# Image 0 loaded and normalised ahead of the tables of relative logits; the taps of the convolution and the second layer's weights asked for last

## The chip, the cores and the metric

The kernel runs on one core of a Trainium2 chip. The metric is the time of one launch in microseconds of the device. Before the change it is 2572.06 us, the median of five runs (2569.28 to 2577.38).

## The reference

A batch of 8 images, 32 x 32 pixels, 256 channels, float32, goes through two layers.

```python
# layer 0: group norm (32 groups), then a hybrid of convolution and attention, and a residual
x = x + concat[ conv3x3(gn(x)) + conv_b   (192 channels),
                attn(gn(x)) @ attn_w + attn_b   (64 channels) ]
#   attn: kqv = gn(x) @ qkv_w + qkv_b; 8 heads of 8; 1024 x 1024 logits per head,
#   logits = q k + rel_w + rel_h     (relative logits from key_rel_w, key_rel_h, 63 x 8 each)
# layer 1: attention of one head of 128 over the 1024 tokens, projected back, two residuals
t = t + (softmax(Q K / sqrt(128)) V) @ W_o + b_o + ln(t)
# then a feed-forward of 2 of 8 experts per image, chosen from the mean token, and a layer norm
t = t + layer_norm(experts(ln(t)) + ln(t)) * gamma + beta
```

## The kernel before, in words

Everything before the experts is one stage with eight rounds, one for each image; the experts are a second stage with eight rounds. In the first stage TensorE's instructions run in the order in which the program lists them (`manual_schedule` for that engine); the other engines' instructions are ordered by the framework's planner, so their order on the chip can differ from the program's. Within one engine instructions run in order, and one that waits holds all behind it.

The part in question is the head, ahead of image 0's first scores.

- *Loads.* `load_image(0)` (L105) loads image 0, 1 MB, on POOL's queue. ScalarE's queue loads `qkvw` (L121, 192 KB) and the convolution's `taps` (L125, 1728 KB). SP's queue loads in this order: `kqb`, `vb`, `l0b` in two parts, `aw`, the three of `wqkv1`, `wo`, `bo` (L139 to L158), and then the two raw tables `rawh` and `raww` (L181, 2 KB each).
- *Taps.* The 3 x 3 convolution is computed for pairs of pixels from sums and differences of the taps: three VectorE operations, a scaling, and two ScalarE copies make `convw` (L130 to L135).
- *Selectors* made of the identity: `gsel`, `gavg`, `esel`, `hsel`.
- *Tables.* For each of the two raw tables: a VectorE copy `rep` (L185), a TensorE transpose `relt` (L187), four VectorE writes (L194) to `bdh` or `bdw`. Then `reld`: 16 pieces, half on VectorE and half on POOL (L205, L208).
- *Key patterns.* `oh` on VectorE (L220 to L222) and 32 POOL operations that fill `km0` and `km1` (L228, L229).
- *Image 0's normalisation,* `norm_steps(0)`: 16 transposes (L270), copies to `xT` (L271), statistics (L275 to L296, with one square root on ScalarE), and the normalised, padded image `gpad` (L299, two VectorE operations). In between POOL adds the bias `l0b` to the image (L279).
- `by_tiles`: POOL copies `gpad` to tiles `x` (L320). `by_pairs`: `gdif`, sums and differences of neighbouring pixels, half on VectorE and half on POOL (L311).
- `input_steps(0)`: matmuls `pk` (L334), ScalarE and VectorE write `kq` (L343, L346), SP's queue writes the keys into `km` (L358, 16 transfers), matmuls `pvv` (L367) that read the tiles `x`, matmuls `prel` (L406) that read `bdw`, then `reld`, evicted to `rw` and `rh` (L418, L420), `rw` sent to DRAM (`rwd`, L423), transposes `tpw` (L431), and unit 0's loads of `F` (L484, L488, L495).
- Then the rounds. Each image has four units of 8 steps, each with scores `lg` (L512) whose maximum VectorE takes (L520), weights `st` (L552) and sums `po` (L569); the convolution's matmuls `pc` (L452), which read `convw` and `gdif`, fill in, and so does the next image's normalisation near the end of a round.

TensorE's order in the head is: relth, reltw, image 0's transposes and the statistics' two small matmul pairs, pk, pvv, prel, tpw, pc. The tiles `taps`, `x`, `rw` and `F` share three buffers; `rep`, `bdh` and `xT` share four.

Of the kernel before, what the change touches and what calls it, by code (L numbers as in the profile page):

```python
# [9 lines left out]
FP = mybir.dt.float32  # L10
I32 = mybir.dt.int32
AF = mybir.ActivationFunctionType
ALU = mybir.AluOpType
# [3 lines left out]
P = 128  # L17
# [3 lines left out]
KC = C // P  # L21
NH, DH, DK = 8, 8, 64
HG = 4
NG = NH // HG
CO = C - DK
U = 128
E, F = 8, 512
# [8 lines left out]
def kernel(  # L36
# [26 lines left out]
    nc = tc.nc  # L63
    xt = x.rearrange("b h w c -> b (h w) c")
# [12 lines left out]
    ident = const.tile([P, P], FP, tag="ident", name="ident")  # L77
# [13 lines left out]
    with ExitStack() as ph:  # L91
        wp = ph.enter_context(tc.tile_pool(name="wp", bufs=1))
        work = ph.enter_context(tc.tile_pool(name="work", bufs=1))
# [8 lines left out]

        def load_image(b):
            t = work.tile([P, NT, C], FP, tag="T", name="T", bufs=2)
            nc.gpsimd.dma_start(out=t.rearrange("p (r j) c -> p r j c", j=2), in_=xt[b].rearrange("(r p j) c -> p r j c", p=P, j=2))  # L105
            return t

        T = {0: load_image(0)}
# [7 lines left out]
        def st_tile(name):  # L116
            return ps_st.tile([P, 512], FP, tag="st", name=name)


        qkvw = wp.tile([P, KC, 3 * DK], FP, tag="qkvw", name="qkvw")  # L120
        nc.scalar.dma_start(out=qkvw, in_=qkv_w.rearrange("(k p) o -> p k o", p=P))  # L121


        taps = work.tile([P, 4096], FP, tag="F", name="taps", bufs=3)[:, 0 : 9 * KC * CO]
        nc.scalar.dma_start(  # L125
            out=taps.rearrange("p (n o) -> p n o", o=CO), in_=conv_w.rearrange("a b (k p) o -> p (a b k) o", p=P)
        )
        taps = taps.rearrange("p (a b n) -> p b a n", a=3, b=3)
        convw = wp.tile([P, 4, 3, KC * CO], FP, tag="convw", name="convw")
        nc.vector.tensor_tensor(convw[:, 2], taps[:, 0], taps[:, 2], ALU.add)  # L130
        nc.vector.tensor_tensor(convw[:, 0], convw[:, 2], taps[:, 1], ALU.add)
        nc.vector.tensor_tensor(convw[:, 1], convw[:, 2], taps[:, 1], ALU.subtract)
        nc.vector.tensor_scalar(convw[:, 0:2], convw[:, 0:2], 0.5, None, ALU.mult)
        nc.scalar.copy(convw[:, 2], taps[:, 0])
        nc.scalar.mul(convw[:, 3], taps[:, 2], -1.0)  # L135
        convw = convw.rearrange("p v a (k o) -> p v a k o", o=CO)

        kqb = wp.tile([P, 1], FP, tag="kqb", name="kqb")
        nc.sync.dma_start(out=kqb, in_=qkv_b[0 : 2 * DK].rearrange("(p o) -> p o", o=1))  # L139
# [7 lines left out]
        l0b = wp.tile([P, 1, C], FP, tag="l0b", name="l0b")  # L147
        nc.sync.dma_start(out=l0b[:, 0, 0:CO], in_=conv_b.partition_broadcast(P))
        nc.sync.dma_start(out=l0b[:, 0, CO:C], in_=attn_b.partition_broadcast(P))
        aw = wp.tile([DK, DK], FP, tag="aw", name="aw")  # L150
        nc.sync.dma_start(out=aw, in_=attn_w)
        wqkv1 = wp.tile([P, 3, KC, U], FP, tag="wqkv1", name="wqkv1")
# [3 lines left out]
        nc.sync.dma_start(out=wo, in_=w_o)  # L156
        bo = wp.tile([P, 1, C], FP, tag="bo", name="bo")
        nc.sync.dma_start(out=bo[:, 0, :], in_=b_o.partition_broadcast(P))  # L158

# [11 lines left out]
        hsel = wp.tile([P, HG], FP, tag="hsel", name="hsel")  # L173
        nc.vector.tensor_reduce(hsel, esel.rearrange("p (h d) -> p h d", d=DH), AX.X, ALU.add)


        rel = []
        for n, table in (("h", key_rel_h), ("w", key_rel_w)):
            M = table.shape[0]
            raw = wp.tile([M, DH], FP, tag=f"raw{n}", name=f"raw{n}")  # L180
            nc.sync.dma_start(out=raw, in_=table)  # L181
            rep = work.tile([P, 2048], FP, tag="pt", name=f"rep{n}", bufs=4)[0:M, 0:P].rearrange(
                "m (r d) -> m r d", d=DH
            )
            nc.vector.tensor_copy(rep, raw.unsqueeze(1).to_broadcast([M, P // DH, DH]))  # L185
            pt = st_tile(f"relt{n}")
            nc.tensor.transpose(pt[:, 0:M], rep.rearrange("m r d -> m (r d)"), ident[0:M, 0:M])  # L187
            if n == "h":
                bd = work.tile([P, 2048], FP, tag="pt", name="bdh", bufs=4)[:, 0 : M * HG]
                bd = bd.rearrange("p (m h) -> p m h", h=HG)  # L190
            else:
                bd = wp.tile([P, M, HG], FP, tag="bdw", name="bdw")
            for h in range(HG):
                nc.vector.tensor_scalar(bd[:, :, h], pt[:, 0:M], hsel[:, h : h + 1], None, ALU.mult)  # L194
            rel.append(bd)
        bdh, bdw = rel
        bdw = bdw.rearrange("p m h -> p (m h)")

        def half_w(rows, m, k):
            return bdw[rows, (m + 16 * k) * HG : (m + 16 * k + 16) * HG]  # L200


        NM = 48
        reld = wp.tile([P, NM, 16, HG], FP, tag="reld", name="reld")
        nc.gpsimd.tensor_copy(reld[:, :, 0, :], bdh[:, 0:NM, :])  # L205
        for j in range(1, 16):
            eng = nc.vector if j % 2 else nc.gpsimd
            eng.tensor_tensor(reld[:, :, j, :], bdh[:, j : j + NM, :], bdh[:, 0:NM, :], ALU.subtract)  # L208
        reld = reld.rearrange("p m j h -> p m (j h)")

        def half_h(rows, m, k):
            return reld[rows, m + 16 * k, :]

        KM = []
        oh = wp.tile([P, 16 + DH], FP, tag="oh", name="oh")
        nc.vector.tensor_copy(oh[:, 0:1], esel[:, 0:1])  # L220
        nc.vector.tensor_tensor(oh[:, 1:16], esel[:, 1:16], esel[:, 0:1].to_broadcast([P, 15]), ALU.add)
        nc.vector.tensor_copy(oh[:, 16:24], esel[:, 24:32])  # L222
        for i in range(NG):
            km = wp.tile([P, 2, 4, P], FP, tag=f"km{i}", name=f"km{i}")
            for a in range(2):
                kv = km[:, a].rearrange("p g (y x) -> p g y x", y=8)
                for g in range(4):
                    nc.gpsimd.tensor_copy(kv[:, g], oh[:, 0:16].unsqueeze(1).to_broadcast([P, 8, 16]))  # L228
                    nc.gpsimd.tensor_tensor(  # L229
                        kv[:, g], kv[:, g], oh[:, 16:24].unsqueeze(2).to_broadcast([P, 8, 16]), ALU.add  # L230
                    )
            KM.append(km)

        mcols = []
        for i in range(2):
# [21 lines left out]

        def f_tile(name):
            return work.tile([P, 2, 4, 512], FP, tag="F", name=name, bufs=3)


        def norm_steps(b):
# [50 lines left out]
        def by_tiles():  # L313

            xn = f_tile("x").rearrange("p a e s -> p (a e s)")[:, 0 : KC * S]
            xn = xn.rearrange("p (k j t) -> p k j t", k=KC, j=NT)
            for kc in range(KC):
                for a in range(2):
                    for e in range(4):
                        nc.gpsimd.tensor_copy(  # L320
                            xn[:, kc, a * 4 + e].rearrange("p (y x) -> p x y", y=8),
                            gpad[:, kc, 1 + 16 * a : 17 + 16 * a, 1 + 8 * e : 9 + 8 * e],
                        )
            return dict(xn=xn)
# [551 lines left out]
        with tc.manual_schedule(engines={mybir.EngineType.PE}):  # L876
            held = {}
            for _ in norm_steps(0):
                pass
            held.update(by_tiles())  # L880
            by_pairs()
            for _ in input_steps(0, held):
                pass
            conv = Conv(0)
            means = []
            for b in range(B):
                last = b + 1 == B
                if not last:
                    T[b + 1] = load_image(b + 1)

                def early():
                    if means:
                        token_mean(*means.pop())

                def ahead():

                    yield from norm_steps(b + 1)
                    held.update(by_tiles())
                    by_pairs()

                now, held = held, {}
                conv.place[0] = st_tile
                conv_layer_attention(
                    b,
                    *(now[k] for k in ("units", "kq", "rh", "rwd", "rwq")),
                    conv,
                    early,
                    iter(()) if last else ahead(),
                )
                conv = Conv(b + 1)  # L910
                steps = iter(()) if last else input_steps(b + 1, held)

                def fill(us):

                    while us > 0:
                        took, small = next(steps, (None, None))
                        if took is None:
                            break
                        us -= took
                        if small:  # L920
                            conv.run(3)

                means.append((b, *attention_layer(b, fill, conv.whole)))
                fill(1000.0)
                del T[b]
            token_mean(*means.pop())
# [268 lines left out]
```

## Time and profile before

| | us |
|---|---|
| median of five runs | 2572.06 |
| the profiled execution | 2578.39 |
| its span, first to last instruction | 2576.6 |
| TensorE busy (share of the span) | 2432.7 (94%) |
| VectorE busy | 1412.1 (55%) |
| ScalarE busy | 977.4 (38%) |
| POOL busy | 407.9 (16%) |
| image 0's load issued | 1.50 |
| taps landed, by the wait that ends with them | 16.59 |
| first transpose of image 0 | 20.20 |
| first pk | 46.65 |
| first load of F issued | 67.24 |

The profile is of one execution; times within it are counted from its first instruction. Busy times count instructions, not transfers. The chain of work that ended last is followed back from the last instruction to whatever released each step, and in it a transfer appears as "DMA". A wait is named after what released it last. In rows of a tile or of a line the three durations are the least, the median and the largest, in ns; the three times from DMA to landing are in us.

### The profile page before, as it was taken

How to read it: one execution, taken by the hardware profiler on the slowest of the kernel's cores; microseconds unless marked ns; L12 is line 12 of the kernel's file. 1: busy time of each engine (PE TensorE's matmuls, PEld its weight loads, DVE VectorE, ACT ScalarE, POOL GpSimd, SP SyncE). 2: the span in 40 equal slices, each digit the busy share in tenths (PEclk: the TensorE clock that was granted, in tenths of full speed). 3: DMA queues.
4: the chain of work that ended last, by engine and by line, in shares of the span. 5: the costliest groups of instructions: out<-in, count | busy, mean ns of one | idle time of the engine just before them, and what ended most of it. 6: DMA issues, size and time to landing. Idle time of an engine off the chain costs nothing.

```text
span 2576.6 us, 42566 instructions
## 1 busy us (share of the span) xinstructions
PE 2432.7 (94%) x17769; PEld 1379.8 (54%) x17769; DVE 1412.1 (55%) x2507; ACT 977.4 (38%) x1617; POOL 407.9 (16%) x440
## 2 busy tenths in 40 slices
PE   3999999999999999999999999999998599999998
PEld 2734753575356436643763376347534366666665
DVE  5575477447744873586367537754772623333332
ACT  1055325532643363346225622553264222222222
POOL 6002120302030103202120212030201211111110
PEclk9899999989999999999999999999998799999999
DMA  2430242024203410440044024302420302112100
GB/s 81 90 62 6 51 94 42 23 34 100 37 22 58 86 26 22 83 80 7 28 93 69 3 48 89 52 7 50 83 37 2 108 28 70 72 72 72 66 37 21
DMA packets 73518, 135.87 MB, mean 53 GB/s; under 512 B 12000, under 2 KB 24168, under 8 KB 71280
## 3 DMA queue, kind: packets, MB, share of 16 engines
q1 hardware_dynamic: 67408, 114.42, 21.2%
q0 software_dynamic: 3328, 16.78, 1.9%
q8 instruction: 140, 2.29, 0.4%
q10 hardware_dynamic: 2592, 1.97, 0.3%
q14 instruction: 50, 0.41, 0.1%
HBM read 53.43 MB, written 25.17 MB: 31 GB/s over the span
## 4 chain that ended last, share of the span: by engine, by line
PE 85%; DVE 7%; ACT 4%; DMA 3%; issue 1%; POOL 0%; ACTq 0%; DVEq 0%; SPq 0%
PE lg L512 15%; PE pc L452 10%; PE po L569 9%; PE py L1125 9%; PE phd L1107 9%; PE st L552 8%; PE po L784 4%; PE lg L753 3%; PE prel L406 3%; PE pq L716 2%; PE tp L773 2%; DVE my L520 2%; DMA F<-mb 2%; PE py L1122 2%; ACT PT L560 1%; PE pk L334 1%
## 5 line engine op out<-in xcount | busy, mean ns | idle before, releaser
L560 ACT ACTIVATE PT<-st 128x512 f32<-128x512 f32 (+1 forms) x944 | 541.6, 633 | 582.2 <-PE st L552 579.8
L520 DVE TENSOR_REDUCE my<-lg 128x32 f32<-128x1024 f32 x512 | 617.8, 1223 | 160.6 <-PE st L552 126.5
L552 PE MATMUL st<-F,km 32*128 32x512 f32 x2048 | 549.2, 638 | 14.6 <-DMA F<-mb 8.8
L512 PE MATMUL lg<-km,F 24*128 24x512 f32 x2048 | 528.0, 637 | 0.9 <-DMA F<-rh 0.9
L452 PE MATMUL pc<-convw,gdif 128*128 128x192 f32 x1536 | 308.7, 344 | 10.6 <-DVE T L467 10.6
L569 PE MATMUL po<-PT,vall 128*32 128x256 f32 (+1 forms) x3200 | 313.5, 451 | 3.0 <-ACT PT L560 2.4
L452 PEld LDWEIGHTS pc<-convw,gdif 128*128 128x128 f32 x1536 | 250.8, 193 | 79.8 <-issue 73.4
L512 PEld LDWEIGHTS lg<-km,F 24*128 24x128 f32 x2048 | 151.6, 183 | 176.4 <-issue 101.7
L1125 PE MATMUL py<-w,hT 128*128 128x256 f32 x1024 | 237.3, 385 | 0.0
L569 PEld LDWEIGHTS po<-PT,vall 128*32 128x32 f32 x3200 | 66.8, 108 | 313.9 <-issue 279.1
L552 PEld LDWEIGHTS st<-F,km 32*128 32x128 f32 x2048 | 179.3, 183 | 91.5 <-issue 41.7
L1107 PE MATMUL phd<-n2T,w 128*128 128x512 f32 x512 | 224.1, 595 | 0.0
L1125 PEld LDWEIGHTS py<-w,hT 128*128 128x128 f32 x1024 | 189.9, 190 | 45.6 <-issue 22.4
L1132 DVE TENSOR_TENSOR r<-py,n 128x256 f32<-128x256 f32 x64 | 27.2, 425 | 310.9 <-PE py L1125 310.9
L279 POOL TENSOR_TENSOR T<-T,l0b 128x2048 f32<-128x2048 f32 x8 | 36.2, 4521 | 815.0 <-PE tpx L270 815.0
L1107 PEld LDWEIGHTS phd<-n2T,w 128*128 128x128 f32 x512 | 97.2, 191 | 115.2 <-issue 108.0
L784 PE MATMUL po<-pt,qkv 128*128 128x256 f32 x512 | 116.6, 381 | 11.3 <-DVE pt L776 11.3
L1114 ACT ACTIVATE hT<-phd,b1c 128x512 f32<-128x512 f32 x128 | 86.4, 686 | 96.8 <-PE phd L1107 96.7
L753 PE MATMUL lg<-qkv 128*128 128x512 f32 x256 | 119.1, 593 | 0.0
L762 DVE TENSOR_REDUCE nm<-lg 128x1 f32<-128x1024 f32 x64 | 78.0, 1219 | 72.5 <-PE lg L753 72.5
L784 PEld LDWEIGHTS po<-pt,qkv 128*128 128x128 f32 x512 | 96.6, 190 | 36.2 <-DVE pt L776 13.2
L701 POOL TENSOR_TENSOR T<-T,n 128x256 f32<-128x256 f32 x64 | 47.1, 742 | 290.7 <-DVE n L696 290.7
(229 smaller groups left out, 2434.5 us busy)
## 6 DMA issues: line engine op xcount, KB each, us to landing
F<-rh SPq DMA_DIRECT2D x256, 128.0 KB
F<-kq SPq DMA_DIRECT2D x256, 64.0 KB
F<-rwd SPq DMA_DIRECT2D x256, 64.0 KB
w<-in_L_ffn_W_dram SPq DMA_DIRECT2D x32, 512.0 KB
T<-in_x_dram POOLq DMA_DIRECT2D x8, 1024.0 KB, 6.0
rwd<-rw SPq DMA_DIRECT2D x16, 512.0 KB
Td<-T POOLq DMA_DIRECT2D x8, 1024.0 KB, 8.0
T<-Td SPq DMA_DIRECT2D x8, 1024.0 KB
```

The lines of the kernel that those rows point to most:

```text
L452: nc.tensor.matmul(pc[:, v, :], lhsT=gflat[:, 2 * pair + v, kc, at : at + P], rhs=convw[:, 2 * pair + v, dy, kc, :], start=i == 0, stop=i ...
L512: nc.tensor.matmul(lg[:, a, :], lhsT=self.F[r : r + 24, a, 0, i * P : (i + 1) * P], rhs=KM[self.g][r : r + 24, a].rearrange("p e k -> p (e ...
L520: nc.vector.tensor_reduce(my[:, :, hl], lg.rearrange("p a (y x) -> p y a x", y=WW), AX.XY, ALU.max)
L552: nc.tensor.matmul(st[:, i, :] if len(heads) > 1 else st, lhsT=KM[self.g][r : r + 32, a, e, :], rhs=self.F[r : r + 32, a, e, :], start=Tru ...
L560: nc.scalar.activation(self.pts[j][:, hs, :], st, AF.Exp)
L569: nc.tensor.matmul(self.po[32 * hl : 32 * hl + 32, cols], lhsT=vall[:, j, h * (DH + 1) : h * (DH + 1) + 32], rhs=self.pts[j][:, hl, cols], ...
L753: nc.tensor.matmul(lg[:, h, :], lhsT=qk[0][:, i * P : (i + 1) * P], rhs=qk[1][:, h * 512 : (h + 1) * 512], start=True, stop=True,)
L762: nc.vector.tensor_reduce(nm, lg, AX.X, ALU.max, negate=True)
L784: nc.tensor.matmul(po[:, 0:IB], lhsT=v1[:, jc, :], rhs=pt[:, jc, :], start=jc == 0, stop=jc == NT - 1)
L1107: nc.tensor.matmul(phd, lhsT=ws[k][0][:, kc, f * P : (f + 1) * P], rhs=n2T[:, kc, q * 512 : (q + 1) * 512], start=kc == 0, stop=kc == KC - 1,)
L1114: nc.scalar.activation(hT[:, k * NF + f, :], phd, AF.Gelu, bias=b1c[:, f, k * B + b : k * B + b + 1])
L1125: nc.tensor.matmul(py, lhsT=hT[:, k * NF + f, j * P : (j + 1) * P], rhs=ws[k][1][:, f, :], start=False, stop=k == TOPK - 1 and f == NF - 1,)
```

## The change

Image 0's load goes to SP's queue and is its first; the other seven images' loads stay on POOL's. The raw tables' loads go to ScalarE's queue, ahead of `qkvw`. The taps' load comes behind `qkvw` and, in the program, behind SP's loads of the small biases; the loads of `aw`, the second layer's weights and the rest follow it. The tables, the key patterns and the taps' arithmetic become functions that are called later: the tables after `norm_steps(0)`, the key patterns after `by_tiles()`, the taps' arithmetic after `input_steps(0)`. What each computes is the same. TensorE's order in the head is now: image 0's transposes and the statistics' matmuls, relth, reltw, pk, pvv, prel, tpw, pc.

```diff
         def load_image(b):
             t = work.tile([P, NT, C], FP, tag="T", name="T", bufs=2)
-            nc.gpsimd.dma_start(out=t.rearrange("p (r j) c -> p r j c", j=2), in_=xt[b].rearrange("(r p j) c -> p r j c", p=P, j=2))
+            eng = nc.gpsimd if b else nc.sync
+            eng.dma_start(
+                out=t.rearrange("p (r j) c -> p r j c", j=2), in_=xt[b].rearrange("(r p j) c -> p r j c", p=P, j=2)
+            )
             return t
...
+        raws = []
+        for n, table in (("h", key_rel_h), ("w", key_rel_w)):
+            raw = wp.tile([table.shape[0], DH], FP, tag=f"raw{n}", name=f"raw{n}")
+            nc.scalar.dma_start(out=raw, in_=table)
+            raws.append((n, raw))
         qkvw = wp.tile([P, KC, 3 * DK], FP, tag="qkvw", name="qkvw")
         nc.scalar.dma_start(out=qkvw, in_=qkv_w.rearrange("(k p) o -> p k o", p=P))
-        taps = work.tile([P, 4096], FP, tag="F", name="taps", bufs=3)[:, 0 : 9 * KC * CO]
-        nc.scalar.dma_start(
...
-        convw = convw.rearrange("p v a (k o) -> p v a k o", o=CO)
...
         nc.sync.dma_start(out=l0b[:, 0, CO:C], in_=attn_b.partition_broadcast(P))
+        taps = work.tile([P, 4096], FP, tag="F", name="taps", bufs=3)[:, 0 : 9 * KC * CO]
+        nc.scalar.dma_start(
+            out=taps.rearrange("p (n o) -> p n o", o=CO), in_=conv_w.rearrange("a b (k p) o -> p (a b k) o", p=P)
+        )
         aw = wp.tile([DK, DK], FP, tag="aw", name="aw")
         nc.sync.dma_start(out=aw, in_=attn_w)
...
+        def tables():
...
+            for n, raw in raws:
...
+            return half_w, half_h
+        def key_patterns():
...
+            return KM
+        def conv_weights(taps):
...
+            return convw.rearrange("p v a (k o) -> p v a k o", o=CO)
...
             for _ in norm_steps(0):
                 pass
+            half_w, half_h = tables()
             held.update(by_tiles())
+            KM = key_patterns()
             by_pairs()
             for _ in input_steps(0, held):
                 pass
+            convw = conv_weights(taps)
             conv = Conv(0)
```

The bodies of the three new functions are the moved lines, unchanged but for the tables' load, which is now made above.

More of the change, by code (lines that the diff above doesn't have):

```diff
@@ L117, in st_tile @@
             return ps_st.tile([P, 512], FP, tag="st", name=name)
+        raws = []
[3 more added lines that the diff above has]
+            raws.append((n, raw))
         qkvw = wp.tile([P, KC, 3 * DK], FP, tag="qkvw", name="qkvw")
         nc.scalar.dma_start(out=qkvw, in_=qkv_w.rearrange("(k p) o -> p k o", p=P))
-        taps = work.tile([P, 4096], FP, tag="F", name="taps", bufs=3)[:, 0 : 9 * KC * CO]
-        nc.scalar.dma_start(
[L126 to L135, printed above, removed]
-        convw = convw.rearrange("p v a (k o) -> p v a k o", o=CO)
         kqb = wp.tile([P, 1], FP, tag="kqb", name="kqb")
@@ L174 @@
         nc.vector.tensor_reduce(hsel, esel.rearrange("p (h d) -> p h d", d=DH), AX.X, ALU.add)
[L177 to L232, printed above, removed]
@@ L259, in f_tile, with half_w, half_h @@
             return work.tile([P, 2, 4, 512], FP, tag="F", name=name, bufs=3)
+        def tables():
+            rel = []
+            for n, raw in raws:
+                M = raw.shape[0]
+                rep = work.tile([P, 2048], FP, tag="pt", name=f"rep{n}", bufs=4)[0:M, 0:P].rearrange(
+                    "m (r d) -> m r d", d=DH
+                )
+                nc.vector.tensor_copy(rep, raw.unsqueeze(1).to_broadcast([M, P // DH, DH]))
+                pt = st_tile(f"relt{n}")
+                nc.tensor.transpose(pt[:, 0:M], rep.rearrange("m r d -> m (r d)"), ident[0:M, 0:M])
+                if n == "h":
+                    bd = work.tile([P, 2048], FP, tag="pt", name="bdh", bufs=4)[:, 0 : M * HG]
+                    bd = bd.rearrange("p (m h) -> p m h", h=HG)
+                else:
+                    bd = wp.tile([P, M, HG], FP, tag="bdw", name="bdw")
+                for h in range(HG):
+                    nc.vector.tensor_scalar(bd[:, :, h], pt[:, 0:M], hsel[:, h : h + 1], None, ALU.mult)
+                rel.append(bd)
+            bdh, bdw = rel
+            bdw = bdw.rearrange("p m h -> p (m h)")
+            def half_w(rows, m, k):
+                return bdw[rows, (m + 16 * k) * HG : (m + 16 * k + 16) * HG]
+            NM = 48
+            reld = wp.tile([P, NM, 16, HG], FP, tag="reld", name="reld")
+            nc.gpsimd.tensor_copy(reld[:, :, 0, :], bdh[:, 0:NM, :])
+            for j in range(1, 16):
+                eng = nc.vector if j % 2 else nc.gpsimd
+                eng.tensor_tensor(reld[:, :, j, :], bdh[:, j : j + NM, :], bdh[:, 0:NM, :], ALU.subtract)
+            reld = reld.rearrange("p m j h -> p m (j h)")
+            def half_h(rows, m, k):
+                return reld[rows, m + 16 * k, :]
+            return half_w, half_h
@@ new lines, in key_patterns @@
+        def key_patterns():
+            KM = []
+            oh = wp.tile([P, 16 + DH], FP, tag="oh", name="oh")
+            nc.vector.tensor_copy(oh[:, 0:1], esel[:, 0:1])
+            nc.vector.tensor_tensor(oh[:, 1:16], esel[:, 1:16], esel[:, 0:1].to_broadcast([P, 15]), ALU.add)
+            nc.vector.tensor_copy(oh[:, 16:24], esel[:, 24:32])
+            for i in range(NG):
+                km = wp.tile([P, 2, 4, P], FP, tag=f"km{i}", name=f"km{i}")
+                for a in range(2):
+                    kv = km[:, a].rearrange("p g (y x) -> p g y x", y=8)
+                    for g in range(4):
+                        nc.gpsimd.tensor_copy(kv[:, g], oh[:, 0:16].unsqueeze(1).to_broadcast([P, 8, 16]))
+                        nc.gpsimd.tensor_tensor(
+                            kv[:, g], kv[:, g], oh[:, 16:24].unsqueeze(2).to_broadcast([P, 8, 16]), ALU.add
+                        )
+                KM.append(km)
+            return KM
@@ new lines, in conv_weights @@
+        def conv_weights(taps):
+            taps = taps.rearrange("p (a b n) -> p b a n", a=3, b=3)
+            convw = wp.tile([P, 4, 3, KC * CO], FP, tag="convw", name="convw")
+            nc.vector.tensor_tensor(convw[:, 2], taps[:, 0], taps[:, 2], ALU.add)
+            nc.vector.tensor_tensor(convw[:, 0], convw[:, 2], taps[:, 1], ALU.add)
+            nc.vector.tensor_tensor(convw[:, 1], convw[:, 2], taps[:, 1], ALU.subtract)
+            nc.vector.tensor_scalar(convw[:, 0:2], convw[:, 0:2], 0.5, None, ALU.mult)
+            nc.scalar.copy(convw[:, 2], taps[:, 0])
+            nc.scalar.mul(convw[:, 3], taps[:, 2], -1.0)
+            return convw.rearrange("p v a (k o) -> p v a k o", o=CO)
```

## The prediction

> **What bounds the kernel now.** First the page's table of engines and the windows: TensorE is busy 94% of the span, and from 80 us on nearly without a gap, so what is left to win at small cost is the head, before TensorE's stream of work starts. The change touches only that head. I therefore went to the chain that ended last, in order of time, for the first 80 us.
>
> ```profile
> PE 2432.7 (94%) x17769; PEld 1379.8 (54%) x17769; DVE 1412.1 (55%) x2507; ACT 977.4 (38%) x1617; POOL 407.9 (16%) x440
> ```
> ```profile
> 1.23 15.34 DMA taps<-in_L_conv_conv_w_dram
> ...
> 16.97 2.58 DMA rawh<-in_L_conv_key_rel_h_dram
> ...
> 28.73 3.05 DVE reld L208 x5
> ...
> 40.89 5.71 DVE gpad L299
> ...
> 46.65 6.47 PE pk L334 x8
> 53.12 3.52 PE pvv L367 x32
> ...
> 79.03 4.09 PE lg L512 x6
> ```
>
> Columns: start, length, work. Image 0 does not appear until 32 us: the taps' load comes first, then the table rows, then VectorE's taps and tables. The waits of SP's queue show why a 2 KB table lands at 19.6 us, and the rows of tile T that the image had been there for long:
>
> ```profile
> SPq L158 <- DMA taps<-in_L_conv_conv_w_dram: 9.6, 1, 9.6
> ```
> ```profile
> DMA to landing us min/median/max: 6.1/9.0/12.0
> ```
>
> Two image loads lie in that answer's window: the one of 45.98 us, alone on the engines, took 6.1 us; the first, issued at 1.50 us beside the taps, 12.0 us. So image 0 landed at 13.5 us and its first transposes ran at 20.20 us, because relth's transpose stands ahead of them in TensorE's written order and waits for reph. Then VectorE did taps and tables until 31.92 us. The timeline of the first 60 us (start, length, engine, work) gives the rest of the path:
>
> ```profile
> 31.92 2.34 DVE L271 COPY xT<-tpx 128x1024 f32<-128x1024 f32 x2
> ...
> 41.55 4.49 POOL L279 TENSOR_TENSOR T<-T,l0b 128x2048 f32<-128x2048 f32 x1
> ...
> 46.89 6.46 POOL L320 COPY x<-gpad 128x128 f32<-128x128 f32 x16
> ```
> ```profile
> 224.92 1.54 DVE L299 TENSOR_SCALAR gpad<-xT,gm,gr 128x1024 f32<-128x1024 f32 x2
> ```
> ```profile
> 52.50 11.57 SPq L358 DMA_DIRECT2D km<-kq  x16
> 64.17 2.46 SPq L423 DMA_DIRECT2D rwd<-rw  x2
> 67.24 0.68 SPq L484 DMA_DIRECT2D F<-rh  x1
> ```
>
> The second fence is image 1, where POOL's addition of l0b was over in time: both gpad writes took 1.54 us. In image 0 they took 5.71 us on the chain, since POOL's 4.49 us addition ran beside them. The third fence is SP's queue: 16 km writes, 2 rwd, then unit 0's loads of F from 67.24 us; its sixteenth is issued by 78.75 us and lg at 79.03 us had waited for F. This start of F, 67.24 us, is my yardstick: what is behind it (11.5 us of issues, the scores, 2490 us of steady work) is unchanged and moves as one.
>
> **The change, part by part.** *Image 0's load* goes from POOL's queue to the head of SP's, issued at about 0.73 us. Bounds of its landing: 0.73 + 6.1 = 6.8 us if nothing competes, 0.73 + 12.0 = 12.7 us if the taps compete as before. The windows show 132, 223, 344, 371 GB/s in the 2 us steps from 2 to 10 us, 2.14 MB by 10 us; image (1.05 MB), qkvw (0.2) and as much of the taps as of the image make 2.3 MB. I take 10 us. One rule speaks against any gain here: the Trainium skill, "DMA: Bandwidth & Descriptors", section "Queues, rings and completion order", says that all queues use the same 16 engines, each taking queues in turn by packet, so a new queue buys no bandwidth. The trace's 12.0 against 6.1 us fits; by the rule alone the image would land at 12.7 us and the forecast below would be 2.7 us later.
>
> *Other loads moved.* raw tables and qkvw go first on ScalarE's queue (three issues of 0.3 to 0.5 us): landed before the image, cover complete. kqb, vb and l0b queue behind the image on SP; l0b is first needed by POOL's addition, after the image's transposes. SP's aw, wqkv, wo and bo may wait for the image or the taps, as bo did for 9.6 us; SP is next needed for km at about 34 us, so 0, and if that cover went it would be the overrun itself. The taps' issue on ScalarE may wait for the image's landing in the same way; queued behind it there is only the square root of the norm, at 21 us. POOL loses a 0.95 us issue in a stretch where it then idles 17 us: 0.
>
> *Image 0's normalisation goes ahead of the tables*, step by step with before's durations: landing 10; eight transposes at 0.22 us (9 took 2.18) to 11.9; copies and statistics 5.04 us (31.92 to 36.96) to 16.9; group statistics 3.93 us (36.96 to 40.89) to 20.9. In their gaps VectorE's planned order may place short ready work: four bdh writes (0.88 us) or one taps addition (1.34 us), the taps landing at about 17 us. Bounds 0 and 2.2; I take 1.3, one such piece: 22.2. gpad takes 1.54 us if POOL's addition is over (it can start when the transposes end, 13.6 us), or lasts until 25.3 us if POOL does its km patterns first (9.56 us from 9.7 us, then 4.49). Taken: 24.5 us. Before it was 46.6, so pk starts 22.1 us sooner.
>
> *The tables come after it*, and give some back. VectorE: bdw and eight reld (26.48 to 31.70, 5.2 us), gdif 3.0 us, then kq 1.07 us: the first half of kq is ready 9.3 us after gpad, at 33.8; before it was 5.8 us after (52.42). SP then needs 11.57 us for km and 1.4 to 3.1 us for rwd: F starts at 46.8 to 48.5. POOL: reld 5.05 us, then the tiles x 6.46 us: done at 36.0, pvv done about 0.6 us later, and prel to rh takes 10.6 us (56.64 to 67.24): F starts at 47.2. Both arms give about 48, so 19 us gained. The relth and reltw transposes on TensorE, 0.36 us each, now lie while it waits for gpad: 0.
>
> *Km patterns* (9.56 us on POOL) were under VectorE's statistics; their operands are ready early, so POOL's idle time from 9.7 us takes most of them. A tail behind the tiles x would hold SP's km writes: 0 to 4 us, I take 1, most of the idle time fitting them.
>
> *Taps' arithmetic* (5.4 us of VectorE, 2.3 us of ScalarE) is needed by the first pc. VectorE is busy 4.2, 1.7 and 2.1 us in the three 10 us windows from 50 to 80, so it is hidden there; ahead of kq it would cost 5.4. I take 1.
>
> *TensorE's clock.* The granted clock is 0.50 from 59.5 to 76 us and from 80 to 85.5. The weight loads of pk show it was low at the first pk too, which the clock column, 1.00 there, does not say:
>
> ```profile
> L334 PEld LDWEIGHTS pk<-gpad,qkvw x8: 288/337/338, 46.6 to 51.9; 128*128 128x128 f32 x8
> L334 PEld LDWEIGHTS pk<-gpad,qkvw x8: 186/188/189, 242.3 to 245.0; 128*128 128x128 f32 x8
> ```
>
> The eight pk took 6.47 us against some 3.4 in image 1. The same matmuls follow the same idle start after the change, so I take 0, with 3.1 us either way as the bound, one pk stage at the other clock. The skill's "TensorE: Matmul & The Clock Gate", Part 1, has the gate open after about 3.4 us of activity in a window that runs freely: by it, too, the slow start is not saved but moves, with a chance phase.
>
> Sum: 19 - 1 - 1 = 17 us. The profiled execution took 2578.39 us (span 2576.6 and 1.8 around it) and would take 2561.4; it is 6.3 us above the median of the five runs, 2572.06, of which 17 us less is 2555.
>
> **The rivals.** *VectorE waits for the taps.* If the planned order keeps the taps' additions ahead of the first xT copy, as before, VectorE stands until 16.6 us and works 5.4 more: copies at 22.0, not 11.9. Ten of the 17 us go, one or two come back as the taps no longer cost later: gain 8, 2564 us. For it: before's order did this, and the taps' load is still issued among the first. Against: in the program the taps now stand behind everything of image 0, and before they ran in program order with it.
>
> *The tables in series.* The rival above, and POOL doing all km patterns between reld and the tiles x: 9.56 us more on the arm that had 47.2. Of the 8 us nothing is left: 2571 to 2573, no change. Against: their operand, oh, needs only ident, and POOL has nothing else at 10 us.
>
> *Steady order worsens: slower.* Only TensorE's order is written; the other engines' orders are planned for the whole stage, and other starting times may reorder VectorE later. Its max over the scores is close to TensorE (54.3 of 70 us busy from 130 to 200). One such reduction, 1.23 us, out of place in each of the 32 units costs 39 us: 2572 - 17 + 39 = 2594. It decides for slower from 0.7 us a unit (22 us). For it: lg waits for VectorE in the waits already. Against: the program behind the head is untouched, and the units' operands tie the order.
>
> **How the numbers follow.** My case 0.74, taps first 0.12, in series 0.07, steady order 0.07. My case's ends: the image at 6.8 us, no piece in the gaps, and gpad undisturbed make 5 us more; the image at 12.7, a km tail and taps ahead of kq make up to 10 less; the clock 3 either way, not all together: 2549 to 2566. With most of the first rival the range is 2549 to 2567. Under 0.2% (5.1 us) a measurement can't tell from no change: faster is my case and most of the first rival, 0.84; same 0.09; slower 0.07.
>
> **What would show it.** Right: taps gone from the chain; first transposes at about 10 us, ahead of relth; gpad ending near 24.5 us and undisturbed or nearly; km writes from 34 us; F's loads from near 48 us; the rest moved as one. Taps first: VectorE idle until taps at 16 us, xT copies after them. Series: POOL's km between reld and x. Wrong altogether: F's loads near 48 us and yet no shorter span.

## The result, and the profile after

The changed kernel takes 2568.04 us (median of 52 runs, 2563.16 to 2590.84), the kernel before 2572.68 us in the same comparison (94 runs, 2566.98 to 2593.8). The ratio is 0.9987, with a 95% interval of 0.9978 to 0.9995: 1.3 to 5.7 us faster, where 17 were forecast. Most of that interval lies within the 0.2% (5.1 us) that the prediction called no change, and the time is 1 us above its range.

The profiled execution after took 2563.78 us (span 2562.0). The busy times have hardly moved, so what changed is idle time:

```profile
PE 2428.0 (95%) x17769; PEld 1378.2 (54%) x17769; DVE 1408.5 (55%) x2507; ACT 977.1 (38%) x1617; POOL 411.7 (16%) x439
```

The chain of waits, in order of time (start, length, work):

```profile
2.17 12.91 DMA taps<-in_L_conv_conv_w_dram
15.11 1.88 DVE convw L269
16.99 2.27 DVE xT L287 x2
...
21.71 1.53 DVE reph L213
...
23.36 1.22 DVE convw L270
...
24.65 1.26 DVE convw L271
...
26.18 1.27 DVE convw L272
...
29.62 2.27 DVE gpad L315 x2
...
32.90 4.53 POOL reld L236 x7
37.43 4.37 POOL x L336 x9
...
41.84 5.33 PE pvv L383 x30
47.17 10.44 PE prel L422 x384
```

The taps head the chain as before. The first of their operations on VectorE (L269) stands ahead of the copies of image 0, which therefore start at 16.9 us, though the image was there long before. The first transposes, which wait for the image, and the waits of SP's queue:

```profile
6.35 3.33 PE L286 MATMUL tpx<-ident,T 128*128 128x128 f32 x16 [6.35 <-DMA T<-in_x_dram]
```
```profile
SPq L153 <- DMA taps<-in_L_conv_conv_w_dram: 6.0, 1, 6.0
```

Issued at 0.73 us, the image had landed by 6.35 us, 5.6 us later, when TensorE began to transpose it; VectorE, ready at 8.64 us, then stood 6.47 us for the taps. The other three of the taps' operations lie among the group statistics, after 23.36 us. SP's own wait for the taps, 6.0 us, cost nothing, as assumed: its next work of image 0 comes at 41.56 us. POOL in the same stretch (timeline: start, length, engine, line, work):

```profile
11.28 4.50 POOL L295 TENSOR_TENSOR T<-T,l0b 128x2048 f32<-128x2048 f32 x1 [2.73 <-DMA l0b<-in_L_conv_attn_b_dram]
15.72 1.66 POOL L258 COPY km<-oh 128x128 f32<-128x128 f32 x2
...
22.79 3.28 POOL L258 COPY km<-oh 128x128 f32<-128x128 f32 x2
26.04 2.04 POOL L259 TENSOR_TENSOR km<-km,oh 128x128 f32<-128x128 f32 x2
...
30.43 0.97 POOL L106 DMA_DIRECT2D T<-in_x_dram  x1
```

The addition of `l0b` waits 2.73 us for its operand, the key patterns come behind it and run from 15.72 to 30.43 us, 14.7 us for work that took 9.56 us before. Two copies that take 0.52 us elsewhere took 3.28 us here, beside VectorE's additions of the taps. POOL is free at 31.40 us and `bdh`, for which it waits next, is written at 32.3: two arms, that is, chains of work that feed the same next step, which end within a microsecond of each other. SP's queue gives the end of the head:

```profile
41.56 12.10 SPq L374 DMA_DIRECT2D km<-kq  x16
55.27 1.75 SPq L439 DMA_DIRECT2D rwd<-rw  x2
58.35 0.68 SPq L500 DMA_DIRECT2D F<-rh  x1
```

F's first load comes at 58.35 us, 8.9 us sooner than before, where 19 were forecast.

### The profile page after: what moved, and what is told of

The parts are those of the page before. It is cut to its first block, busy times and chain, and to the rows that moved or that the text cites. A ratio compares the mean times of both kernels' runs of the same rounds, so it can differ in the third digit from the quotient of the medians.

```text
span 2562.0 us, 42565 instructions
## 1 busy us (share of the span) xinstructions
PE 2428.0 (95%) x17769; PEld 1378.2 (54%) x17769; DVE 1408.5 (55%) x2507; ACT 977.1 (38%) x1617; POOL 411.7 (16%) x439
## 4 chain that ended last, share of the span: by engine, by line
PE 84%; DVE 7%; ACT 4%; DMA 3%; issue 1%; POOL 0%; SPq 0%; ACTq 0%; DVEq 0%
PE lg L528 15%; PE pc L468 10%; PE po L585 9%; PE py L1144 9%; PE phd L1126 9%; PE st L568 8%; PE po L800 4%; PE lg L769 3%; PE prel L422 3%; PE pq L732 2%; PE tp L789 2%; DVE my L536 2%; DMA F<-mb 2%; PE py L1141 2%; ACT PT L576 1%; PE pa L812 1%
## 5 line engine op out<-in xcount | busy, mean ns | idle before, releaser
L568 PE MATMUL st<-F,km 32*128 32x512 f32 x2048 | 550.4, 640 | 14.7 <-DMA F<-mb 8.8
```

Of the source, the lines that this page charges most:

```text
L568: nc.tensor.matmul(st[:, i, :] if len(heads) > 1 else st, lhsT=KM[self.g][r : r + 32, a, e, :], rhs=self.F[r : r + 32, a, e, :], start=Tru ...
```

## The experiments

The theory: the change is worth what was forecast once the taps' arithmetic stays out of image 0's way, and two things hold it, the taps on VectorE and the bias and key patterns on POOL. The rivals: that the loads' places alone matter, that the order of work alone matters, and that the gain is lost behind the head. Each run's ratio is its time over that of the kernel before in the same comparison. In the table, from the timelines: the first copy `xT`, the end of `gpad`, the end of the last tile `x`, F's first load and the start of the third group of `pc` matmuls (us). From there on VectorE, ScalarE and POOL run the same instructions in the same order in all thirteen profiles.

| kernel | xT | gpad | x | F | pc |
|---|---|---|---|---|---|
| before | 31.92 | 47.39 | 53.35 | 67.24 | 88.87 |
| before, again (e1) | 31.45 | 46.91 | 52.88 | 66.00 | 88.29 |
| after | 16.92 | 31.89 | 43.62 | 58.35 | 79.65 |
| after, again (e2) | 16.66 | 31.64 | 43.35 | 59.77 | 81.30 |
| e3, taps late | 8.56 | 19.94 | 32.57 | 48.86 | 71.12 |
| e4, taps and bias late | 8.56 | 21.73 | 33.28 | 49.96 | 70.62 |
| e5, taps behind the copies | 8.55 | 25.52 | 41.76 | 57.84 | 80.01 |
| e6, before with raw tables first | 29.76 | 39.71 | 53.40 | 69.48 | 91.93 |
| e7, order alone | 25.97 | 38.59 | 50.13 | 64.98 | 86.58 |
| e8, both late, placed better | 8.55 | 20.59 | 32.13 | 47.45 | 69.17 |
| e9, bias late alone | 19.45 | 31.68 | 42.72 | 55.24 | 77.23 |
| e10, e5 and bias late | 8.56 | 28.34 | 39.43 | 53.73 | 75.48 |
| e11, e3 with the image on POOL's queue | 13.86 | 23.79 | 42.67 | 58.75 | 80.18 |

**Both kernels again (e1, e2).** No edit.

> The kernel before, unchanged, for a second profile. Its first profile had F's first load at 67.24 us, the after kernel's at 58.35: 8.9 us apart, yet the runs are only 3 to 5 us apart. Theory A (the head's length is fixed, the runs scatter by what happens later): F's first load again within 1 us of 67.2, the eighteen-matmul pc group after it within 1 us of 83.1, and another set of half-clock stretches later than 500 us. Theory B (the head of before was unluckily long in that one profile, by the phase of TensorE's clock): F's first load 3 to 5 us sooner, at 62 to 64 us.

> The changed kernel, unchanged, for a second profile and a second comparison with the kernel before. Theory A: F's first load within 1 us of 58.4 and the time 4 to 9 us below before's. Theory B: F's first load moves by more than 2 us with the place of the half-clock stretches; the time 3 to 5 us below.

The kernel before against itself: 2572.06 us against 2578.22, ratio 0.9987 (0.9968 to 1.0005). The changed kernel: 2571.42, ratio 0.9964 (0.9943 to 0.9985). Medians of one kernel move by some 6 us between groups of runs. Short stretches in which TensorE is granted half its clock (0.50 in the profile) lie in other places from run to run. F's first load moved by 1.2 and 1.4 us between two profiles of one kernel, a little more than theory A's 1 us and less than theory B asks; smaller differences at F between two single profiles show nothing. One such stretch lies in the profiled execution of before; the windows (length, busy times and counts of PE, PEld, DVE, ACT, POOL, then the granted clock, the share of the DMA engines and GB/s) show it, before first and after second:

```profile
500.00:550.00 50.00, 48.25 (x589) 37.55 (x588) 14.39 (x25) 10.14 (x17) 7.45 (x5) 0.86 0.08 27
```
```profile
500.00:550.00 50.00, 48.90 (x495) 35.47 (x495) 19.67 (x36) 15.20 (x26) 4.45 (x1) 1.00 0.25 56
```

A clock of 0.86 over 50 us is 7 us of lost clock. From the third `pc` group to the end of the span are 2487.7 us in this profile, 2481.7 in e1, 2482.3 after and 2482.1 in e2: apart from such a stretch, the rest of the kernel takes the same time. Over all thirteen profiles this part of the span takes 2480 to 2492 us; less half of the time that the trace's clock record has at 0.50, it is 2450 to 2453 us in every one. Profile against profile the head gained 7.0 (e1 to e2) and 9.2 us; the medians show 4.6 in the first comparison and, in the second, 6.8 against the 23 runs of before and less than 1 against e1's twelve.

**Taps late (e3).** The taps' arithmetic is issued behind the last write of `kq`.

```diff
-                nc.vector.tensor_scalar(
+                mark["kq"] = nc.vector.tensor_scalar(
...
-            convw = conv_weights(taps)
+            with tc.issue_after(mark["kq"].ins):
+                convw = conv_weights(taps)
```

> The changed kernel with the four VectorE operations on the taps queued behind the second write of kq, so that none stands ahead of the image's first copy. Theory 1 (VectorE's wait for the taps at 15.1 us is the step that failed): xT's first copy at 8.5 to 9 us instead of 16.9, gpad written by 19 to 22 us instead of 31.9, F's first load at 44 to 47 us instead of 58.4, and the time 11 to 14 us below the changed kernel's. Theory 2 (POOL's chain, km, reld and the tiles x, is the bound and VectorE's wait is hidden behind it): F's first load at 54 us or later, the time less than 5 us below the changed kernel's.

2555.82 us, ratio 0.9923 (0.9894 to 0.9952). VectorE's timeline:

```profile
8.56 1.16 DVE L289 COPY xT<-tpx 128x1024 f32<-128x1024 f32 x1
...
18.12 1.82 DVE L317 TENSOR_SCALAR gpad<-xT,gm,gr 128x1024 f32<-128x1024 f32 x2
...
36.33 6.04 DVE L271 TENSOR_TENSOR convw<-taps 128x1152 f32<-128x1152 f32 x1
42.29 1.01 DVE L436 COPY rw<-prel 128x512 f32<-128x512 f32 x1
```

One edit, on VectorE's order alone, brings the forecast time. `gpad` is done 12 us sooner than after the change, as theory 1 has it, and F starts 9.5 us sooner, 2 us behind that theory's range. The planner's order for POOL changed with it: with `gpad` early, its copies to `x` came ahead of half of the key patterns, which no longer hold them. What is left on the path is L271: 6.04 us instead of 1.34, and `rw` behind it.

**Taps and bias late (e4).** e3, and image 0's addition of `l0b` is issued behind POOL's last copy to `x`.

```diff
-            nc.gpsimd.tensor_tensor(T[b], T[b], l0b.to_broadcast([P, NT, C]), ALU.add)
+            if b:
+                nc.gpsimd.tensor_tensor(T[b], T[b], l0b.to_broadcast([P, NT, C]), ALU.add)
...
+            with tc.issue_after(mark["x"].ins):
+                nc.gpsimd.tensor_tensor(T[0], T[0], l0b.to_broadcast([P, NT, C]), ALU.add)
```

> As the one before, and POOL's 4.5 us addition of l0b to image 0 queued behind the tiles x, so that the key patterns take POOL's idle time instead. Theory 1 with a POOL arm as predicted: key patterns done by 19 to 20 us, gpad by 20 us, tiles x by 32, F's first load at 43 to 45 us, 0 to 3 us sooner than with the taps late alone. If POOL's chain was the bound all along (theory 2): 4 to 5 us sooner than with the taps late alone.

2555.13 us, ratio 0.9908 (0.9879 to 0.9937). F's first load was to come up to 3 us sooner than in e3 and came 1.1 us later; the third `pc` group came 0.5 us sooner. The key patterns now run from 8.72 to 18.3 us, at full speed, but beside the copies and statistics of the image, whose `gpad` ends 1.8 us later than in e3. With the taps gone, the bias is worth nothing more.

**Taps behind the copies only (e5).** As e3, but behind the second copy `xT` of image 0, so that only the taps' wait is taken from the image and their arithmetic stays among its statistics.

```diff
-            convw = conv_weights(taps)
+            with tc.issue_after(mark["xT", 0].ins):
+                convw = conv_weights(taps)
```

> The changed kernel with the taps' arithmetic queued only behind the image's second copy to xT: it no longer stands ahead of the image, but may still fall into the gaps of the statistics. If the wait ahead of the first copy is all that failed: xT's first copy at 8.6 us and F's first load near 50 us, as with the taps behind kq (48.9). If the pieces in the gaps cost as well, each first waiting for the taps at 15.1 us: gpad written at 26 to 28 us, F's first load at 54 to 56 us, about half of the way from 58.4 to 48.9.

2564.8 us, ratio 0.998 (0.9951 to 1.0009). `gpad` is done 6.4 us sooner than after the change, and F starts 0.5 us sooner, later than either theory had it. Its chain:

```profile
14.94 1.66 POOL km L260 x2
...
18.92 2.94 POOL km L261 x2
...
33.35 2.24 POOL x L338 x8
...
40.00 6.66 PE pvv L385 x30
```

All of it is POOL: `l0b`'s landing, the addition, the key patterns from 14.94 to 32.4 us, and only then `x`. The patterns take 17.4 us: of the 7.9 us beyond their undisturbed 9.56, 4.5 lie beside VectorE's additions of the taps and 3.4 beside its work on `gpad`, `reld` and `gdif`. Six microseconds on VectorE were worth next to nothing, because the other arm ended at the same place.

**Bias late alone (e9).** The changed kernel with e4's edit of the addition only; the taps stay where the planner puts them.

> The changed kernel with only POOL's part mended: the addition of l0b to image 0 is queued behind the tiles x, so that the key patterns fill POOL's idle time; the taps' arithmetic stays where the planner put it, one operation ahead of the image's copies and three among the statistics. In the changed kernel VectorE's way to bdh ended at 32.4 us and POOL's key patterns and load at 31.4. Theory M (two arms of nearly one length, each hiding what the other costs): key patterns done by 19 us, gpad at 28 to 30 us, F's first load at 51 to 54 us, so some 5 us sooner than 58.4 and 2 to 4 us short of the version with both mended (49.96). If POOL alone is the bound: F's first load at 48 to 50 us. If VectorE alone: at 57 us or later.

2566.79 us, ratio 0.9971 (0.994 to 1.0001). The key patterns are done at 18.2 us, and `gpad` still ends at 31.7. VectorE, and POOL's last key patterns (timelines):

```profile
15.15 4.37 DVE L271 TENSOR_TENSOR convw<-taps 128x1152 f32<-128x1152 f32 x1 [6.51 <-DMA taps<-in_L_conv_conv_w_dram]
19.45 2.34 DVE L289 COPY xT<-tpx 128x1024 f32<-128x1024 f32 x2
```
```profile
17.53 0.78 POOL L261 TENSOR_TENSOR km<-km,oh 128x128 f32<-128x128 f32 x2
18.23 0.97 POOL L106 DMA_DIRECT2D T<-in_x_dram  x1
```

The first of the taps' operations took 4.37 us, until 1.2 us after POOL's last key pattern; the copies start even later than after the change. Still F comes 3.1 us sooner: POOL, with nothing else left, starts `x` at 31.03 us, ahead of `reld`, so that 18 of `pvv`'s 32 matmuls can run at 38.5 us, where after the change 2 did. F, at 55.24 us, lies between theory M's range and that of VectorE alone.

**Both halves in the weaker form (e10).** e5 with e4's edit of the addition.

> Taps' arithmetic behind the image's second copy but among the statistics, as in the run that had F's first load at 57.84 us, and the addition of l0b to image 0 behind the tiles x. Theory M: with POOL free, what is left of the taps among the statistics, a wait to 15.1 us and 5.4 us of work, puts gpad at 23 to 26 us and F's first load at 49 to 52 us: 6 to 9 us gained by POOL's part here, against 1 us lost by it where the taps were already behind kq (48.86 to 49.96). If the taps among the statistics are the bound by themselves: F's first load at 56 us or later.

2557.96 us, ratio 0.9922 (0.9889 to 0.9955); F at 53.73 us, 1.7 us behind theory M's range and short of the other's. VectorE:

```profile
15.30 4.22 DVE L271 TENSOR_TENSOR convw<-taps 128x1152 f32<-128x1152 f32 x1 [2.82 <-DMA taps<-in_L_conv_conv_w_dram]
...
26.80 1.54 DVE L318 TENSOR_SCALAR gpad<-xT,gm,gr 128x1024 f32<-128x1024 f32 x2
```

Each half alone leaves an interval that reaches 1 (e5, e9); both together give one that ends at 0.9955, as two arms make it. At F the halves alone gain 0.5 and 3.1 us and both 4.6; the 1.0 us beyond their sum is less than the 1.4 us between two profiles of one kernel and shows nothing by itself. Compared with e4, the taps' arithmetic among the statistics costs another 3.8 us at F (6.6 at the end of `gpad`).

**Before, with the raw tables asked for first (e6).** The kernel before with only the two small loads moved to the head of ScalarE's queue.

```diff
+            nc.scalar.dma_start(out=raws[n], in_=table)
...
-            nc.sync.dma_start(out=raw, in_=table)
+            raw = raws[n]
```

> The kernel before with one part of the change alone: the two raw tables are loaded on ScalarE's queue ahead of qkvw, not on SP's behind bo. Theory L (the changed kernel's gain comes from the loads, chiefly from the tables no longer landing at 19.6 us behind the taps): xT's first copy at 26 to 28 us instead of 31.9 and F's first load at 62 to 63 us instead of 67.2 (66.0 in the second profile). Theory O (it comes from the order of work, image before tables): F's first load at 65 us or later, since VectorE still waits for the taps before it does the tables and then the image.

2572.93 us, ratio 0.9999 (0.9983 to 1.0014): F came 2.2 us later than before. That is in theory O's range, but for a reason on POOL that neither theory had. The image's copies came 2.2 us sooner and `gpad` 7.7 us, but POOL's work was planned differently. Its addition and the matmuls that wait for `x` (timeline):

```profile
43.89 4.49 POOL L282 TENSOR_TENSOR T<-T,l0b 128x2048 f32<-128x2048 f32 x1
...
51.64 6.66 PE L370 MATMUL pvv<-qkvw,x 128*128 128x64 f32 x30 [1.55 <-POOL x L323]
```

The key patterns' second halves ran until 43.9 us, the addition until 48.4, and the last `x` came at 53.40 us, where it had been before.

**Order alone (e7).** The changed order of work, with every load issued as before (the image on POOL's queue, the raw tables behind SP's others, the taps behind `qkvw`).

> The other half alone: the changed kernel's order of work with all loads as in the kernel before (image on POOL's queue, taps second on ScalarE's, raw tables last on SP's). All four operations on the taps then stand ahead of the image's copies on VectorE. Theory O: xT's first copy at 22 us (taps 16.6 plus 5.4), F's first load at 59 to 62 us, at least two thirds of the changed kernel's gain. Theory L: F's first load at 64 us or later.

2578.07 us, ratio 1.0002 (0.9987 to 1.0017). All four of the taps' operations came ahead of the image's copies, the second of them beside POOL's addition of `l0b`:

```profile
17.70 5.53 DVE L270 TENSOR_TENSOR convw<-convw,taps 128x1152 f32<-128x1152 f32 x1
```

The copies start at 25.97 us, where theory O had 22, and F's 64.98 us lies in theory L's range, which e6 does not bear out as the cause. So neither the loads (as far as e6 tries them) nor the order is worth anything alone; the head is 2.3 us shorter at F than in the first profile of before and 1.0 us shorter than in e1, which the runs do not show.

**The image back on POOL's queue (e11).** e3 with image 0's load where it was before.

```diff
-            eng = nc.gpsimd if b else nc.sync
+            eng = nc.gpsimd
```

> The version with the taps behind kq, but image 0 loaded on POOL's queue again. It tells what SP's queue and the start ahead of the taps are worth: on SP's queue the image landed 5.9 us after its issue, at 6.6 us, where 10 had been taken. If the queue buys nothing (all queues share the engines): the image lands at 7 to 8.5 us and F's first load stays within 1 us of 48.86. If the start ahead of the taps decides: the image lands at 11 to 13.5 us, xT's first copy at 13 to 15 us, gpad at 23 to 26 us, and F's first load 4 to 8 us later than 48.86.

2571.53 us, ratio 0.9983 (0.9957 to 1.0008); F 9.9 us later than in e3. Its chain:

```profile
1.50 10.24 DMA T<-in_x_dram
...
15.61 4.52 POOL T L297
...
40.91 6.67 PE pvv L385 x30
```

The image takes 10.24 us and not 5.6, and its copies start 5.3 us later, as the second theory has it; F is later than that theory's 4 to 8 us. (The 5.9 us that the expectation names is image 1's load, issued on POOL's queue at 30.43 us; the profile has no landing for the load on SP's queue but what waited for it.) The rest is POOL again: the addition now waits for the transposes, the key patterns end at 33.5 us, and `reld` and `x` stand behind them.

**Both late, placed better (e8).** The taps' arithmetic behind the first copy `rw`, the addition behind POOL's half of `gdif`.

```diff
+            with tc.issue_after(mark["gdif"].ins):
+                nc.gpsimd.tensor_tensor(T[0], T[0], l0b.to_broadcast([P, NT, C]), ALU.add)
...
+            with tc.issue_after(mark["rw"].ins):
+                convw = conv_weights(taps)
```

> The changed kernel with the taps' arithmetic queued behind the first copy of prel to rw, and the addition of l0b to image 0 behind POOL's half of gdif. With the taps behind kq the first taps operation took 6.04 us because POOL's gdif held the port, and the copy to rw behind it came at 42.3 us. Theory 1: the copy to rw comes at 39 to 41 us, F's first load at 46 to 48 us, the time 1 to 3 us below that of the version with taps behind kq (2555.8). If TensorE's clock or SP's queue bounds the stretch from pvv on: F's first load stays at 49 to 50 us and the time within 1 us of it.

2552.96 us, the lowest median, ratio 0.9926 (0.9903 to 0.995), not to be told from e3 and e4 by their intervals; F's 47.45 us is as theory 1 has it. Its chain has no taps ahead of `rw`:

```profile
19.05 1.54 DVE gpad L318 x2
...
35.13 3.61 PE prel L425 x128
38.76 1.11 DVE rw L437
39.87 2.05 DVE convw L271
```

## Why the prediction was wrong

*The step that failed* is the taps' arithmetic, "so it is hidden there ... I take 1", and with it the choice of case. The operations were planned ahead of the image's first copy (one) and among its statistics (three): the prediction's first rival, in a milder form than its "additions ahead of the first xT copy". It had put 2564 us and a chance of 0.12 on it, against 0.74 for its own case. The argument against it was that the program now lists the taps behind everything of image 0. The trace of before already spoke against that argument: there the program lists the taps (L130) ahead of the selectors (L163, L171) and of the tables' copy (L185), and VectorE ran these three first.

```profile
19.57 0.22 DVE L185 COPY reph<-rawh 63x128 f32<-63x128 f32 x1 [19.57 <-DMA rawh<-in_L_conv_key_rel_h_dram]
19.72 0.27 DVE L163 TENSOR_REDUCE gsel<-ident 128x16 f32<-128x128 f32 x1
...
20.19 1.34 DVE L130 TENSOR_TENSOR convw<-taps 128x1152 f32<-128x1152 f32 x1
```

The order on VectorE is the planner's, and a place in the program doesn't bind it; e3 shows what binding it brings, 2555.82 us, where 2555 was forecast for it.

*The image's part.* Landing was taken at 10 us and had come by 6.35; the low bound, 6.8, was nearer. The first copies at 11.9 in the forecast came at 16.9, and at 8.6 where the taps didn't hold them. From the first copy to `gpad`'s end the forecast had 12.6 us; 15.0 were measured after the change, with 3.8 us of taps and 1.5 us of the small copy `reph` in them, and 11.4 in e3. The "1.3" for a short piece in the gaps was the term that the planner overran.

*POOL.* Of the key patterns, "POOL's idle time from 9.7 us takes most of them ... I take 1" failed too, hidden behind the first failure. Two covers were gone: `l0b`, "first needed by POOL's addition, after the image's transposes", was late for it by 2.73 us, and the addition went ahead of the key patterns. These then took 14.7 us for the 9.56 counted, since VectorE's work stood in their way. It would have cost most of the gain without the wait for the taps: in e5 POOL is the whole chain, and F is only 0.5 us sooner. Neither arm shows its price while the other is as long, which is why e5 and e9 gain little and e10, e4 and e8 much more; e3 gains it all with an edit on VectorE alone because POOL's planned order changed too.

*From `x` to F.* The forecast let `pvv` end 0.6 us behind the last `x` and put F 11.2 us behind it. The table has F 12.5 to 16.7 us behind the last `x` in every kernel, 14.7 after the change: `pvv` takes 5.33 us from its ninth tile on, at a granted clock of 0.64 (6.66 in e2, at 0.50; all of it took 3.52 in before, at 1.00), and ends 3.55 us behind `x`. In before, 53.35 to 67.24 us, 13.9, was there to be read. Of the 11.1 us between the 47.2 forecast for this arm and 58.35, 7.6 had arisen by the last `x` and 3.5 arose behind it. In e3, e4 and e8 this overrun is paid for by an image that is normalised 3 to 5 us sooner than forecast, so their 2553 to 2556 us meet the forecast by two errors that cancel.

*What held.* From `gpad` to the km writes 9.3 us were forecast and 9.67 measured (31.89 to 41.56). The yardstick held: from F's first load to the third `pc` group it is 20.7 to 22.5 us in all the kernels of the table. The rival of a worse steady order fell (the order behind the head is the same), and "tables in series" did not happen: key patterns were done before `reld`. The clock's term of 3.1 us either way covers `pk`, which took 5.56 us instead of 6.47; `pvv` it left out.

*Open.* In the profiles the head gains 7 to 9 us; the medians of the first comparison gain 4.6, its lower quartiles 5.4 (2570.65 to 2565.30). Of the 52 runs of the changed kernel 29 lie between 2563 and 2570 us and 23 above, up to 2590.84, so that its median falls at the edge of the lower group. Spans of the kernel before ran from 2567.6 us at a granted clock of 0.986 to 2591.1 us at 0.976 in one comparison, a scatter wider than the change is worth. Where the stretches lie is known only for profiled executions, so what part of the missing 2 to 5 us they make is not settled.

## What to carry to other kernels

When an order is left to a planner, moving a block of code to the end of the program does not move its work to the end: ask which instruction will be ready when, and bind the order where it matters. Two engines that feed the same point must both be followed to the end of the stage, since a saving on one is worth nothing while the other ends at the same time. A price that the trace of before shows for a whole stretch (from the last tile to the first load, 13.9 us) is better than a sum of the parts one believes to be in it.

## What was not expected of the hardware

VectorE and POOL kept each other standing for far longer than one instruction. An addition of the taps takes 1.34 us undisturbed (L131 in before), and took 6.04 us in e3, 5.53 in e7 and 4.37 in e9. In e3 and e9 it ended 1.2 us, nearly its own length, after POOL's unbroken work had ended (at 41.15 and 18.31 us); in e7, 1.2 us after one addition of POOL's had ended, at 22.02 us, while POOL's next two copies stood in their turn. POOL in e3, and in e7:

```profile
37.99 3.16 POOL L329 TENSOR_TENSOR gdif<-gpad 128x512 f32<-128x512 f32 x3
41.04 0.97 POOL L106 DMA_DIRECT2D T<-in_x_dram  x1
```
```profile
17.36 4.66 POOL L295 TENSOR_TENSOR T<-T,l0b 128x2048 f32<-128x2048 f32 x1 [7.67 <-PE tpx L286]
21.96 2.85 POOL L258 COPY km<-oh 128x128 f32<-128x128 f32 x2
```

The other way round, after the change POOL's two key copies stood 3.28 us instead of 0.52 beside two of VectorE's additions in a row. In e4 neither kept the other out for long: two additions took 2.14 and 2.11 us, and POOL's half of `gdif` beside them 6.38 instead of 4.14. What decides between these cases is not shown.

The Trainium skill, "SBUF — State Buffer", section "Who interferes with whom", says that the two engines share a pair of ports as an exclusive lock, and that an operation of VectorE with two inputs in SBUF contends over it with one of POOL that reads SBUF. The runs agree on which operations block each other; for the length, e7 fits a lock that is held for one instruction, POOL's addition of 4.66 us, but e3 and e9 show a whole string of POOL's instructions. In the forecast this would have stretched the key patterns, which it had counted at their undisturbed 9.56 us.

The image's 1 MB landed within 5.6 us at the head of SP's queue with the taps' 1728 KB issued 1.4 us behind it, as fast as image 1's load alone on POOL's queue (6.1 in before, 5.9 after). On POOL's queue it took 10.24 us with the taps 0.6 us behind it (e11), and 12.0 with the taps 0.3 us ahead (before, e7). The prediction set the skill's rule that a new queue buys no bandwidth ("DMA: Bandwidth & Descriptors", "Queues, rings and completion order") against its own 10 us. The landing at 12.7 us that it worked out by that rule was not seen; e11 and e3 differ in the queue and in the lead over the taps, so they do not tell which of the two gave the 4.6 us.
